# Layer 0's scans: from tiles of 2 states x 64 channels to tiles of 4 states x 32 channels, with steps and source rows through DRAM

## The chip, the core and the metric

The kernel is one launch on one core of a Trainium2 chip. TensorE (PE), VectorE (DVE), ScalarE (ACT) and GpSimd (POOL) compute; SyncE (SP) issues every DMA, in program order. The metric is the device time of the launch in microseconds.

## What is computed

A two-layer network in fp32 on `x` of 2 x 2048 x 256. Layer 0 adds to x a selective scan and a mixture of experts, both of the normalised x. Layer 1 adds two Mamba directions with a feed-forward part, and a butterfly network. The scan of layer 0, cut to what matters:

```python
z, params = x @ W_z.T, x @ W_params.T                # e = 256 channels, n = 16 states, r = 64
dt = softplus(params[..., :r] @ W_dt.T + b_dt)       # one step width per time and channel
u = silu(causal_conv(x))                             # per time and channel
A = -exp(A_log)                                      # channel x state
A_tilde = exp(dt[..., None] * A)
B_tilde = where(abs(A) < 1e-5, dt[..., None], (A_tilde - 1) / (A + 1e-10))
h[t+1] = A_tilde[t] * h[t] + B_tilde[t] * u[t]       # one scan per channel and state
y = einsum('bln,blen->ble', C, h)
out = ((y + u * D) * silu(z)) @ W_out.T
```

## The kernel before, in words

**Order.** All work is written as small operations `op(engine, us, f, deps, key, takes)`. A planner (`Plan.order`) sorts them once, at build time, into one order for each engine, from the keys, the costs written beside each operation, ring sizes (`rings`) and PSUM banks (`BANKS`). On the chip each engine then runs its list in order, and so does SyncE with its DMAs: a DMA that waits for a buffer or for a result holds all later ones. `key` counts scans; layer 0 has 32 keys to a chunk.

**Layer 0.** Time is cut into chunks of 512 steps (`T`), four for each of two batches, so eight chunks. Beside the scans of a chunk run the preparation of the next (`prepare`), the gates (`gates`), the output product (`finish`), and, spread over all chunks, the prologues, eight passes of experts (`experts`: gather at L773 and L782, first product L817, second L851, way back L898) and two chains of butterfly products on POOL and DVE.

A chunk's scans work on tiles of 128 partitions x 512 steps, 2 states x 64 channels each. An index `j` from 0 to 15 names a pair of such tiles (`h` = 0, 1), so a chunk has 32 scans. Each pair goes through these steps:

- two DMAs of 64 partitions bring C's rows of the two states (`cb`, L1235), and one brings source factors (`Gm` from the DRAM tile `Gd`, L1239);
- ACT makes the decay exp(dt * A) (L1224) from `dt`, which lies twice in SBUF, once for each state of a tile;
- the source: the recurrence is carried in a form in which the difference of u from step to step, times 1/A, enters (or dt * u, where A is tiny). For one half of the channels (`e` = 0) it is a product on PE with 128 rows (L1251: 64 rows of differences, 64 of shifted dt * u) out of `dw`; for the other half ACT scales `dw` (L1257) and DVE adds `dv` times a factor (L1262);
- DVE scans (L1271); POOL copies the last column (`hn`, L1291) for the next chunk and multiplies by `cb` (L1295);
- PE adds the two states into the sum `y` (L1299): two products, each of 64 columns of the matrix `fold`.

`prepare` makes `par` (L953), `dt` (four products L977, ACT L983, softplus L1051), u (ACT L1030), dt * u (POOL L1073), differences (POOL L1082 and once more L1100) and shifted copies (ACT L1085, L1107). What the changed variable lacks (`lack`, PE L1187, DVE L1190, PE L1194) and u * D (`skip`, ACT L1175) start the sum in PSUM; `gated` (DVE L1311) ends it.

**Layer 1** has sixteen chunks of 64 scans with the same decay, scan, `keep` (`hc`, L2044), product (L2050) and collect (L2062).

Of the kernel before, what the change touches and what calls it, by code (L numbers as in the profile page):

```python
# [99 lines left out]
RING0, CB0, STAGE0, RELAY0, XN0, DT0, DW0, GM0, LEAD0, LOAD0, SOURCE0, PROD0, COLLECT0, AHEAD0 = 5, 3, 4, 2, 3, 3, 4, 2, 4, 6, 2, 1, 3, 4  # L100
EARLY0, GATE0, PREP0, FIN0, PRO0, EXP0, EXP1, BFLY0 = -2, (10, 15), (4,30), (4, 12), ((-1, 8), (4, 14)), (10,27), (122,21), ((8, 110), (114, 200))
# [3 lines left out]
ON_POOL = "RRRRRR"  # L105
BANKS = {"pp0":((3,4,5,6,7),3),"yacc0":((0,1,2),3),"pp":((4,5,6,7),2),"ab":((4,5,6,7),2),"yacc":((0,1,2,3),4)}
# [316 lines left out]
def layer0(tc, c, a, pl, pools, x1d, wupd, wdnd, bupd):  # L423
# [23 lines left out]
    def weights():  # L447
        def first():
            W["cw"] = wp.tile([P, 2, 4], F32, name="cw")
            nc.sync.dma_start(W["cw"], a["conv0"].rearrange("(k p) c -> p k c", p=P))  # L450
            W["wpar"] = wp.tile([P, 2, 112], F32, name="wpar")
            nc.sync.dma_start(W["wpar"], a["wpT"].rearrange("(k p) e -> p k e", p=P))
            W["wdt"] = wp.tile([64, 512], F32, name="wdt")
            nc.sync.dma_start(W["wdt"], a["wdtT"])
            W["bdt"] = wp.tile([P, 4], F32, name="bdt")
            nc.sync.dma_start(W["bdt"], a["dt0"])

        def scans():
            W["A"] = wp.tile([P, 4, NS], F32, name="A")
            nc.sync.dma_start(W["A"], a["A0"])  # L460
            W["As"] = wp.tile([P, 4, 8], F32, name="As")
            nc.sync.dma_start(W["As"], a["A0s"])
            W["D0"] = wp.tile([64, 4], F32, name="D0")
            nc.sync.dma_start(W["D0"], a["D0"])
# [11 lines left out]
        def exps():  # L476
            nc.scalar.activation(W["As"], W["As"], AF.Exp)
            nc.scalar.activation(W["A"], W["A"], AF.Exp)

        def inverse(A, name):  # L480

            n = A.shape[2]
            small = wp.tile([P, 4, n], F32, name=name + "small")
            nc.vector.tensor_scalar(small, A, 1e-5, None, ALU.is_lt)
            large = wp.tile([P, 4, n], F32, name=name + "large")
            nc.vector.tensor_scalar(large, small, -1.0, 1.0, ALU.mult, ALU.add)
            c1 = wp.tile([P, 4, n], F32, name=name + "c1")
# [5 lines left out]
            return c1, small  # L493

        def factors():
            c1, small = inverse(W["A"], "c")

            cf = W["cf"] = wp.tile([P, 4, NS], F32, name="cf")
            nc.vector.tensor_copy(cf[0:64], c1[0:64])
            nc.vector.tensor_copy(cf[64:P], small[64:P])  # L500
            fold = W["fold"] = wp.tile([P, 64], F32, name="fold")
            nc.vector.tensor_add(fold, c.ident[:, 0:64], c.ident[:, 64:P])
            W["Gd"] = c.dram.tile([P, 2, 8, P], F32, name="Gd")

        def rows():
            W["c1s"], W["smalls"] = inverse(W["As"], "r")
            nc.vector.tensor_scalar(W["As"], W["As"], -1.0, None, ALU.mult)

        def sources(h):

            if h == 0:
                W["G"] = fp.tile([P, 4, NS, 64], F32, tag="selT", name="G")
            G = W["G"]
            nc.vector.tensor_mul(
                G[:, h],
                W["fold"].unsqueeze(1).broadcast_to([P, NS, 64]),
                W["cf"][:, h].unsqueeze(2).broadcast_to([P, NS, 64]),
            )

        def store(h):  # L520
            nc.sync.dma_start(
                W["Gd"][:, h].rearrange("p m e -> p (m e)"),
                W["G"][:, h].rearrange("p n e -> p (n e)"),
            )

        def lacks():

            nc.vector.tensor_scalar(W["cf"][0:64], W["cf"][0:64], -1.0, None, ALU.mult)

        def turn():  # L530
            W["ps"] = c.pp()
            for h in range(4):
                nc.tensor.transpose(
                    W["ps"][0:16, h * P : (h + 1) * P], W["cf"][:, h], c.ident
# [32 lines left out]
        f = op(DVE, 2.0, factors, e, key=-38)  # L567
        M["As"] = op(DVE, 1.2, rows, e, key=-30)
        M["G"] = []
        for h in range(2):  # L570
            g = op(DVE, 2.6, lambda h=h: sources(h), f, key=-20 + 6 * h,
                   takes="selT" if h == 0 else ())
            st = op(SP, 0.1, lambda h=h: store(h), g, key=-20 + 6 * h)
            if h == 0:
                g0 = g
            g0.users["selT"].append(st)
            M["G"].append(st)
        k = op(DVE, 0.5, lacks, *M["G"], g, key=-1.9)
        t = op(PE, 0.2, turn, k, key=-1.8, takes="pp0")
# [7 lines left out]
    def prologue(b, q, k0, k1, keep=None):  # L587
# [9 lines left out]
        for h in range(2):  # L597
# [6 lines left out]
            def norm(h=h):  # L604
                v = S["x"][:, 2 * h : 2 * h + 2]
                c.normalize(v, v, *S["m", h], 2, nc.gpsimd if ON_POOL[5] == "R" else None)
# [3 lines left out]
            ns.append(op(*((POOL, 1.5) if ON_POOL[5] == "R" else (DVE, 1.7)), norm, m))  # L610
# [111 lines left out]
    def experts(b, ec, k0, k1, k2):  # L722
# [3 lines left out]
        for q in range(4):  # L726
# [42 lines left out]
            for k in range(2):  # L769
                def gather(q=q, k=k):  # L770
                    S["g", q, k] = c.pp()
                    for i in range(4):
# [3 lines left out]
                            S["pb", q][:, i].rearrange("p g e -> p (g e)"),  # L776
# [4 lines left out]
                def gathered(q=q, k=k):  # L781
                    nc.scalar.copy(  # L782
                        S["selT"][:, k].rearrange("p e g -> p g e")[:, 32 * q : 32 * (q + 1), :],
                        S["g", q, k].rearrange("p (g e) -> p g e", e=16),
# [5 lines left out]
                o = op(ACT, 1.01, gathered, g, fs[0])  # L790
# [130 lines left out]
    class Chunk:  # L921
        def __init__(self, b, ch):
            self.b, self.ch, self.first = b, ch, ch == 0
            self.dt, self.dw, self.y = {}, {}, {}
# [4 lines left out]
    def prepare(i, k0, k1):  # L929
# [28 lines left out]
        def project():  # L958
            nc.scalar.copy(ck.par, S["p"][0:112, :])
            ck.cd = c.dram.tile([NS, T], F32, tag="cd0", name="cd0", bufs=3)  # L960

# [9 lines left out]
        ck.t_dt = {}  # L971
        for h in range(4):
            def delta_mm(h=h):
                if h % 2 == 0:
                    ck.dt[h // 2] = ap.tile([P, 2, T + 1], F32, tag="dt", name="dt", bufs=rings["dt0"])
                S["d", h] = c.pp()
                nc.tensor.matmul(  # L977
                    S["d", h], W["wdt"][:, h * P : (h + 1) * P], ck.par[0:64, :],
# [3 lines left out]
            def delta(h=h):  # L982
                nc.scalar.activation(  # L983
                    ck.dt[h // 2][:, h % 2, 1:], S["d", h], AF.Identity,
                    bias=W["bdt"][:, h : h + 1],
                )

            m = op(PE, 0.98, delta_mm, par, *outs[:h - h % 2], takes=("pp0", "dt0") if h % 2 == 0 else "pp0")
            if h % 2 == 0:
                ck.t_dt[h // 2] = m  # L990
                inline("dt0", m)
                m0 = m
            elif h % 2:
                m.deps.append(m0)
            p.users["par0"].append(m)
            outs.append(op(ACT, 0.63, delta, m))
            m.users["pp0"].append(outs[-1])

# [7 lines left out]
        for e in range(2):  # L1006
# [18 lines left out]
            def silu_u(e=e):  # L1025
                if e == 0:
                    ck.uw = ap.tile([P, 4, T + 2], F32, tag="uw", name="uw", bufs=rings["uw"])
                for h in (2 * e, 2 * e + 1):
                    r = slice(64 * (h % 2), 64 * (h % 2) + 64)
                    nc.scalar.activation(ck.uw[0:64, h, 2:], S["c", e][r], AF.Silu)  # L1030

            o = op(ACT, 1.25, silu_u, o, *us, takes="uw" if e == 0 else (), table="silu")
# [5 lines left out]
        def edge():  # L1038
            uw = ck.uw
            if ck.first:  # L1040
                nc.gpsimd.memset(uw[:, :, 0:1], 0.0)
                nc.gpsimd.tensor_copy(uw[0:64, :, 1:2], uw[0:64, :, 2:3])
# [5 lines left out]
        def softplus():  # L1048
            for e in range(2):
                d = ck.dt[e]  # L1050
                nc.scalar.activation(d[:, :, 1:], d[:, :, 1:], AF.Softplus)  # L1051

        so = op(ACT, 2.05, softplus, *outs, table="softplus")
        ck.o_sp = so
# [1522 lines left out]
```

## Time and profile before

| | |
|---|---|
| median of 3 runs | 2833.63 us (2831.72 to 2835.28) |
| profiled execution, first to last instruction | 2826.7 us |
| what lies around it, by the median | 6.9 us |
| scans of layer 0, first start to last start | 56.8 to 869.7 us |
| mean granted TensorE clock | 0.966 |
| busy over the span | PE 2535.5, DVE 2339.7, ACT 2261.0, POOL 2353.5 us |
| DMA | 282.62 MB, mean 100 GB/s |

A group of the profile reads: line, engine, operation, out<-in by the program's names, partitions x elements, count | busy us, mean ns of one | idle time of the engine just before them, and what ended it. A window gives the busy time of each engine in a stretch, then the granted clock, the mean share of the 16 DMA engines in use and the GB/s. A wait names who waited, for whom, the sum in us, how often, and the longest.

### The profile page before, as it was taken

To read this page: it belongs to the slowest core of one execution; us is meant where nothing else is said; L and a number is where in the kernel's file an instruction comes from. 1 tells how busy PE (TensorE), PEld (TensorE's weight loads), DVE (VectorE), ACT (ScalarE), POOL (GpSimd) and SP (SyncE) were. 2 spreads that over 40 slices of the span, in tenths; PEclk is the share of its full clock that TensorE was granted. 3 is DMA by queue.
4 is the path that set the end of the run, shared out by engine and by line. 5 is a ranking of instruction groups with operands and counts; after the bars stand their busy time and mean duration, and the time that the engine had idled before them with its cause. 6 is when DMAs were issued, how large, how long until landed. Compare 5 with 4: busy or idle time off the path is not lost.

```text
span 2826.7 us, 42579 instructions
## 1 busy us (share of the span) xinstructions
PE 2535.5 (90%) x15008; PEld 1851.1 (65%) x15008; DVE 2339.7 (83%) x2545; ACT 2261.0 (80%) x3460; POOL 2353.5 (83%) x2253
## 2 busy tenths in 40 slices
PE   6767988889986989999999999999999999999996
PEld 2333444444433768787787777878878788787875
DVE  5645886669795889998999999989898898989884
ACT  5747876778875989998898888879889889887871
POOL 6967667886565999998998989989898998988893
PEclk9979999999997999999999999999999999999998
DMA  6445347755433122212222232321212212212221
GB/s 212 135 144 180 119 126 247 258 173 160 139 106 127 50 79 77 90 50 65 68 83 65 75 91 79 96 81 49 73 56 73 79 46 83 60 64 64 62 63 50
DMA packets 228261, 282.62 MB, mean 100 GB/s; under 512 B 22160, under 2 KB 170768, under 8 KB 226128
## 3 DMA queue, kind: packets, MB, share of 16 engines
q1 hardware_dynamic: 228048, 279.91, 31.4%
q8 instruction: 118, 1.93, 0.3%
q14 instruction: 95, 0.78, 0.1%
HBM read 221.38 MB, written 58.46 MB: 99 GB/s over the span
## 4 chain that ended last, share of the span: by engine, by line
PE 51%; DVE 16%; POOL 14%; issue 7%; ACT 7%; DMA 4%; SPq 1%; POOLq 0%; DVEq 0%; ACTq 0%
PE bank L2018 10%; PE bank L2062 8%; POOL a L2050 7%; DVE a L2031 6%; PE bank L2246 3%; PE bank L2203 3%; PE bank L2132 3%; PE bank L1672 3%; POOL a L1295 3%; PE bank L1701 3%; DVE a L1271 2%; PE bank L2314 2%; PE bank L1795 2%; PE bank L1299 2%; POOL bT L1944 2%
## 5 line engine op out<-in xcount | busy, mean ns | idle before, releaser
L2050 POOL TENSOR_TENSOR a<-a,cb 128x1024 f32<-128x1024 f32 x512 | 1217.1, 2377 | 30.0 <-DMA cb<-bcd 0.5
L2031 DVE TENSOR_TENSOR_SCAN a<-a,hc,bank 128x512 f32<-128x512 f32 x768 | 930.7, 1261 | 73.3 <-PE bank L2018 65.6
L2000 ACT ACTIVATE a<-dt,A 128x512 f32<-128x512 f32 x1024 | 678.6, 717 | 53.4 <-PE bank L2062 35.7
L2018 PE MATMUL bank<-ident,bT 128*128 128x128 f32 x4096 | 616.5, 276 | 33.4 <-DVE a L2031 22.2
L2018 PEld LDWEIGHTS bank<-ident,bT 128*128 128x128 f32 x4096 | 486.1, 142 | 182.7 <-issue 68.3
L2062 PE MATMUL bank<-ident,a 128*128 128x128 f32 x4096 | 567.2, 274 | 37.9 <-POOL a L2050 37.5
L2062 PEld LDWEIGHTS bank<-ident,a 128*128 128x128 f32 x4096 | 470.6, 141 | 77.5 <-POOL a L2050 55.0
L1942 ACT ACTIVATE bT<-dtuT,BT 128x512 f32<-128x512 f32 x640 | 424.6, 714 | 13.8 <-PE bank L2018 8.2
L2031 DVE TENSOR_TENSOR_SCAN a<-a,bank 128x512 f32<-128x512 f32 x256 | 295.0, 1202 | 43.0 <-PE bank L2018 39.3
L1295 POOL TENSOR_TENSOR a<-a,cb 128x1024 f32<-128x1024 f32 x128 | 302.4, 2363 | 10.3
L1944 POOL TENSOR_SCALAR bT<-dtuT,BT 128x512 f32<-128x512 f32 x384 | 272.3, 713 | 9.0 <-PE bank L2018 1.8
L1271 DVE TENSOR_TENSOR_SCAN a<-bank,hn,a 128x512 f32<-128x512 f32 x192 | 241.6, 1275 | 35.0 <-PE bank L1251 29.6
L1224 ACT ACTIVATE a<-dt,As 128x512 f32<-128x512 f32 x256 | 173.5, 717 | 22.4 <-PE bank L1299 15.9
L1299 PE MATMUL bank<-a,fold 128*64 128x512 f32 x512 | 148.8, 654 | 22.7 <-POOL a L1295 22.0
L2044 POOL COPY hc<-a 128x2 f32<-128x2 f32 x512 | 107.8, 210 | 73.5 <-DVE a L2031 72.9
L1291 POOL COPY hn<-a 128x2 f32<-128x2 f32 x128 | 26.4, 206 | 168.8 <-DVE a L1271 165.0
L1251 PE MATMUL bank<-dw,Gm 128*128 128x512 f32 x256 | 140.9, 650 | 12.7 <-ACT dw L1085 3.2
L2203 PE MATMUL bank<-xnT,wup 128*128 128x256 f32 x512 | 125.5, 387 | 16.9 <-DMA wup<-wupd 13.9
L2132 PE MATMUL bank<-wout,ygT 128*128 128x256 f32 x512 | 126.7, 381 | 3.6 <-ACT h L2323 3.3
L2246 PE MATMUL bank<-wdn,gff 128*128 128x256 f32 x512 | 128.9, 386 | 0.7 <-ACT yT L2295 0.6
L1672 PE MATMUL bank<-winz,xnT 128*128 128x512 f32 x256 | 124.7, 597 | 4.7 <-DVE zu L1726 2.6
L1701 PE MATMUL bank<-xnT,winx 128*128 128x512 f32 x256 | 122.7, 595 | 1.6 <-DVE zu L1726 1.5
(211 smaller groups left out, 4339.2 us busy)
## 6 DMA issues: line engine op xcount, KB each, us to landing
cb<-bcd SPq DMA_DIRECT2D x256, 256.0 KB, 3.2
xnq<-xnd SPq DMA_DIRECT2D x32, 512.0 KB, 4.5
cb<-cd SPq DMA_DIRECT2D x128, 128.0 KB, 3.0
f<-in_f_dram SPq DMA_DIRECT2D x32, 512.0 KB, 4.8
interd<-stage SPq DMA_DIRECT2D x64, 256.0 KB, 4.8
relay<-interd SPq DMA_DIRECT2D x64, 256.0 KB, 3.3
xnTd<-xnT SPq DMA_DIRECT2D x16, 512.0 KB, 4.4
Gm<-Gd SPq DMA_DIRECT2D x64, 128.0 KB, 2.9
```

The source lines that it names most:

```text
L1271: nc.vector.tensor_tensor_scan(v, R["x", h], v, 0.0 if ck.first else pv.hn[:, k, h : h + 1], ALU.add, ALU.mult,)
L1295: nc.gpsimd.tensor_mul(v, v, C["cb"].unsqueeze(1).broadcast_to([P, 2, T]))
L1942: nc.scalar.activation(t, ck.dtuT[:, q, :], AF.Copy, scale=v)
L1944: nc.gpsimd.tensor_scalar(t, ck.dtuT[:, q, :], v, 1.0, ALU.mult, ALU.mult)
L2000: nc.scalar.activation(R["a"][:, h], ck.dt[:, e0 + h], AF.Exp, scale=w["A"][:, e0 + h, n : n + 1],)
L2018: nc.tensor.transpose(R["b", h][:, q * P : (q + 1) * P], ck.bT[n, q][:, e * P : (e + 1) * P], c.ident,)
L2031: nc.vector.tensor_tensor_scan(v[:, step], v[:, step], b[:, step], 0.0 if ck.first else pv.hn[:, e, n : n + 1], ALU.mult, ALU.add,)
L2050: nc.gpsimd.tensor_mul(v, v, ck.cb[n].unsqueeze(1).broadcast_to([P, 2, T]))
L2062: nc.tensor.matmul(ck.y[e][:, tb * P : (tb + 1) * P], v[:, tb * P : (tb + 1) * P], c.ident, start=False, stop=(n == NS - 1), is_transpose= ...
L2132: nc.tensor.matmul(S["ps"][:, n * D : (n + 1) * D], ck.ygT[:, e, q * P : (q + 1) * P], ck.w["wout"][:, e, :], start=(e == 0), stop=(e == 3),)
L2203: nc.tensor.matmul(S["up", hp][:, j * 256 : (j + 1) * 256], FW["wup"][:, kk, hd * P : (hd + 1) * P], ck.xnT[:, kk, t0 : t0 + 256], start=( ...
L2246: nc.tensor.matmul(S["ps"][:, j * D : (j + 1) * D], S["g"][:, hd, j * P : (j + 1) * P], FW["wdn"][:, hd, :], start=(hd == 0), stop=(hd == 7),)
```

## The change

Layer 0's tiles become 4 states x 32 channels; a chunk still has 32 scans in 16 pairs, now half of the channels after the other (`e` = j // 8).

- `dt`, softplus, u and dt * u are made once for 128 channels, without the doubled halves. The chunk's `dt` is stored to a DRAM tile `dd`, and for each 32 channels loaded back four times over (`dr`). Differences and dt * u are stored to a DRAM tile `wd` and loaded back as 64-row pairs (`w4`). The shifted copies, the second subtraction and the DRAM tile `Gd` go; the factors `G` stay in SBUF.
- Every source is a product with 64 rows, two side by side on the two row halves (`source`); `scaled` and `rest` go.
- C's rows come in one DMA for four states, and serve two pairs.
- The collect takes two pairs at once, four products of 32 columns each into four parts of the bank.
- `skip` and the adding of `lack` move from ACT and PE to DVE.
- `keep` is left out in the last chunk of each sequence, in layer 0 and in layer 1.
- In the experts, the gather product reads `pb` with the expert outermost, and ACT writes `selT` from it in runs of eight.
- Banks and rings: six banks for layer 0's products and sources (`pp0`, `ab0`, up to four for sources), two for sums; `dt` one buffer, `dr` five, `w4` three; the preparation lies on keys 1 to 24.

The core of the diff:

```diff
-RING0, CB0, STAGE0, RELAY0, XN0, DT0, DW0, GM0, LEAD0, LOAD0, SOURCE0, PROD0, COLLECT0, AHEAD0 = 5, 3, 4, 2, 3, 3, 4, 2, 4, 6, 2, 1, 3, 4
-EARLY0, GATE0, PREP0, FIN0, PRO0, EXP0, EXP1, BFLY0 = -2, (10, 15), (4,30), (4, 12), ((-1, 8), (4, 14)), (10,27), (122,21), ((8, 110), (114, 200))
+RING0, CB0, STAGE0, RELAY0, XN0, DR0, W40, LEAD0, LOAD0, SOURCE0, PROD0, COLLECT0, AHEAD0 = 5, 3, 4, 2, 3, 5, 3, 4, 6, 2, 1, 3, 4
+EARLY0, GATE0, PREP0, FIN0, PRO0, EXP0, EXP1, BFLY0 = -2, (10, 15), (1,24), (4, 12), ((-1, 8), (4, 14)), (10,27), (122,21), ((8, 110), (114, 200))
-ON_POOL = "RRRRRR"
-BANKS = {"pp0":((3,4,5,6,7),3),"yacc0":((0,1,2),3),"pp":((4,5,6,7),2),"ab":((4,5,6,7),2),"yacc":((0,1,2,3),4)}
+ON_POOL = "RR"
+BANKS = {"pp0":((2,3,4,5,6,7),3),"yacc0":((0,1),2),"pp":((4,5,6,7),2),"ab":((4,5,6,7),2),"ab0":((2,3,4,5,6,7),4),"yacc":((0,1,2,3),4)}
+            W["As"] = W["A"][:, 96:P].rearrange("p (g m) -> p g m", m=4)
+            W["D0"] = wp.tile([P, 2], F32, name="D0")
...
+            W["As"] = W["A"][:, 96:P].rearrange("p (g m) -> p g m", m=4)
+            fold = W["fold"] = wp.tile([P, 32], F32, name="fold")
+            W["G"] = wp.tile([P, 64, 32], F32, name="G")
...
-                            S["pb", q][:, i].rearrange("p g e -> p (g e)"),
+                            S["pb", q][:, i].rearrange("p g e -> p e g"),
...
-                        S["selT"][:, k].rearrange("p e g -> p g e")[:, 32 * q : 32 * (q + 1), :],
-                        S["g", q, k].rearrange("p (g e) -> p g e", e=16),
+                        S["selT"][:, k, :, 32 * q : 32 * (q + 1)].rearrange("p e (i g) -> p i e g", g=8),
+                        S["g", q, k].rearrange("p (i e g) -> p i e g", e=16, g=8),
-                o = op(ACT, 1.01, gathered, g, fs[0])
+                o = op(ACT, 0.6, gathered, g, fs[0])
...
+            ck.dd = c.dram.tile([D, T], F32, tag="dd0", name="dd0", bufs=3)
+            ck.wd = c.dram.tile([8, 2, 32, T], F32, tag="wd0", name="wd0", bufs=3)
...
+            nc.scalar.activation(ck.dt[:, :, 1:], ck.dt[:, :, 1:], AF.Softplus)
...
+        ck.o_dd = op(
+            lambda: nc.sync.dma_start(ck.dd.rearrange("(e p) t -> p e t", p=P), ck.dt[:, :, 0:T]),
+            ed,
+        )
...
+        def delta_u():
+            nc.gpsimd.tensor_mul(ck.uw[:, 2:4, 2:], ck.dt[:, :, 1:], ck.uw[:, 0:2, 2:])
...
-                (nc.gpsimd if ON_POOL[1 + e] == "R" else nc.vector).tensor_mul(
-                    ck.uw[64:P, s, 2:], ck.dt[e][0:64, :, 1:], ck.uw[0:64, s, 2:]
-                (nc.gpsimd if ON_POOL[3 + e] == "R" else nc.vector).tensor_sub(dw[0:64], ck.uw[0:64, s, 1 : T + 1], ck.uw[0:64, s, 0:T])
-                nc.scalar.copy(ck.dw[e][64:P], ck.uw[64:P, s, 0:T])
-                    nc.gpsimd.tensor_sub(
-                        ck.dw[1][64:P], ck.uw[0:64, s, 1 : T + 1], ck.uw[0:64, s, 0:T]
-                    nc.scalar.copy(ck.dv[64 * h : 64 * h + 64], ck.uw[64:P, s, 0:T])
+            def keep_v(e=e):
+                nc.sync.dma_start(ck.wd[4 * e : 4 * e + 4, 1], ck.uw[:, 2 + e, 0:T])
+
+            def step_u(e=e):
+                S["dd", e] = ap.tile([P, T], F32, tag="step", name="step", bufs=rings["step0"])
+                nc.gpsimd.tensor_sub(S["dd", e], ck.uw[:, e, 1 : T + 1], ck.uw[:, e, 0:T])
+
+            def keep_d(e=e):
+                nc.sync.dma_start(ck.wd[4 * e : 4 * e + 4, 0], S["dd", e])
...
+            def lack_mm(e=e, R=R):
+
+                for h in range(2):
+                    R[h] = c.pp()
+                for h in range(2):
+                    r = slice(64 + 32 * h, 80 + 32 * h)
+                    nc.tensor.matmul(R[h], W["cl"][r, e], ck.par[r, :], start=True, stop=True)
+
+            def lack_u(e=e, R=R):
                 ck.y[e] = c.yacc()
+                nc.vector.tensor_mul(ck.y[e], R[0], ck.uw[:, e, 1 : T + 1])
+
+            def skip(e=e):
+                nc.vector.scalar_tensor_tensor(
+                    ck.y[e], ck.uw[:, e, 2:], W["D0"][:, e : e + 1], ck.y[e], ALU.mult, ALU.add
+                )
+
+            def lack_v(e=e, R=R):
+                R["t"] = sp.tile([P, T], F32, tag="lk", name="lk", bufs=rings["lk"])
+                nc.vector.tensor_mul(R["t"], R[1], ck.uw[:, 2 + e, 1 : T + 1])
+
+            def lack_add(e=e, R=R):
+                nc.vector.tensor_add(ck.y[e], R["t"], ck.y[e])
...
-            m, e = divmod(j, 2)
-            k = 8 * e + m
+            e, g, jj = j // 8, j % 8 // 2, j % 2
+            jp = 2 * e + jj
...
+                def load_dt(h, jp=jp, Q=Q):
+                    Q["dt", h] = ap.tile([P, T], F32, tag="dr", name="dr", bufs=rings["dr0"])
+                    cg = 2 * jp + h
+                    nc.sync.dma_start(
+                        Q["dt", h],
+                        ck.dd[32 * cg : 32 * cg + 32].unsqueeze(0).broadcast_to([4, 32, T]),
+                    )
+
+                def load_w(jp=jp, Q=Q):
+                    Q["w"] = ap.tile([P, T], F32, tag="w4", name="w4", bufs=rings["w40"])
+                    nc.sync.dma_start(
+                        Q["w"], ck.wd[2 * jp : 2 * jp + 2].rearrange("g k p t -> (g k p) t")
+                    )
+
+                for h in range(2):
+                    Q["o_dt", h] = op(SP, 0.1, lambda load_dt=load_dt, h=h: load_dt(h), ck.o_dd,
+                                      takes="dr0", key=key - LOAD0 - 1 + h)
+                    inline("dr0", Q["o_dt", h])
+                Q["o_w"] = op(SP, 0.1, load_w, *ck.o_wd[e], takes="w40", key=key - LOAD0)
+                inline("w40", Q["o_w"])
...
+                def load(g=g, C=C):
+                    C["cb"] = sp.tile([P, T], F32, tag="cb", name="cb", bufs=rings["cb0"])
+                    nc.sync.dma_start(
+                        C["cb"],
+                        ck.cd[4 * g : 4 * g + 4].unsqueeze(1).broadcast_to([4, 32, T]),
+                    )
+
+                ld = op(SP, 0.1, load, ck.o_cd, takes="cb0", key=key - LOAD0)
+                inline("cb0", ld)
...
-            if e == 0:
-                C = {}
-
-                def load(m=m, C=C):
-                    C["cb"] = sp.tile([P, T], F32, tag="cb", name="cb", bufs=rings["cb0"])
-                    for j in range(2):
-                        nc.sync.dma_start(
-                            C["cb"][64 * j : 64 * j + 64], ck.cd[2 * m + j].partition_broadcast(64)
-                        )
-                    C["G"] = sp.tile([P, 2, P], F32, tag="G", name="Gm", bufs=rings["G"])
-                    nc.sync.dma_start(C["G"], W["Gd"][:, :, m, :])
-
-                ld = op(SP, 0.2, load, ck.o_cd, *M["G"], takes=("cb0", "G"), key=key - LOAD0)
-                inline("cb0", ld)
...
+            def source(g=g, jp=jp, R=R, Q=Q):
+                for h in range(2):
+                    R["x", h] = c.ab()
+                for h in range(2):
+                    r = slice(64 * h, 64 * h + 64)
+                    nc.tensor.matmul(
+                        R["x", h],
+                        W["G"][r, 16 * jp + 4 * g : 16 * jp + 4 * g + 4].rearrange("p n e -> p (n e)"),
+                        Q["w"][r], start=True, stop=True,
+                    )
+
+            s = op(PE, 1.0, source, Q["o_w"], M["G"], takes=("ab0", "ab0"), key=key - SOURCE0)
...
-                def source(h=h, R=R, C=C):
-                    R["x", h] = c.ab()
-                    nc.tensor.matmul(
-                        R["x", h], C["G"][:, h, :], ck.dw[0][:, h, :], start=True, stop=True
-                    )
-
-                def scaled(h=h, m=m, R=R):
-                    R["x", h] = c.ab()
-                    nc.scalar.activation(
-                        R["x", h], ck.dw[1][:, h, :], AF.Copy, scale=W["c1s"][:, 2 + h, m : m + 1]
-                    )
-
-                def rest(h=h, m=m, R=R):
-                    nc.vector.scalar_tensor_tensor(
-                        R["x", h], ck.dv[:, h, :], W["smalls"][:, 2 + h, m : m + 1], R["x", h],
-                        ALU.mult, ALU.add,
-                    )
-
...
+            if ck.ch < NT - 1:
+                kp = ck.o_keep[j] = op(POOL, 0.3, keep, before, key=key + 1 - PROD0)
...
-            def collect(e=e, m=m, R=R):
-                for h in range(2):
-                    nc.tensor.matmul(
-                        ck.y[e][64 * h : 64 * h + 64], W["fold"], R["a"][:, h], start=False,
-                        stop=(m == 7), skip_group_check=True,
-                    )
...
+                def collect(e=e, g=g, quad=quad):
+                    for q in range(4):
+                        nc.tensor.matmul(
+                            ck.y[e][32 * q : 32 * q + 32], W["fold"], quad[q // 2][0]["a"][:, q % 2],
+                            start=False, stop=(g == 3), skip_group_check=True,
+                        )
+
+                cl = op(PE, 1.05, collect, *prods, *ck.o_sum[e], key=key + 1 + COLLECT0)
...
+            self.last = k == (0 if self.bw else NT - 1)
+                if not ck.last:
+                    kp = op(POOL, 0.24, keep, sc[1], key=at + k + 1 - PROD)
```

## The prediction

> **What bounds the kernel now.** First the page's chain of work that ended last, then one window over the layer 0 stage (0 to 871 us; the last of its scans ends there) with two of its chunks.
>
> ```profile
> PE 51%; DVE 16%; POOL 14%; issue 7%; ACT 7%; DMA 4%; SPq 1%; POOLq 0%; DVEq 0%; ACTq 0%
> ```
> ```profile
> 0.00:871.00 871.00, 710.80 (x3088) 348.10 (x3088) 616.07 (x756) 640.04 (x976) 615.02 (x517) 0.93 0.52 165
> ```
> ```profile
> 500.00:603.00 103.00, 92.71 (x476) 49.63 (x476) 66.03 (x74) 84.03 (x124) 89.75 (x65) 1.00 0.70 227
> 603.00:709.00 106.00, 94.02 (x459) 50.81 (x460) 91.27 (x99) 89.58 (x148) 67.76 (x52) 0.95 0.54 171
> ```
>
> The columns are busy us of PE, PE weight loads, DVE, ACT and POOL, then the granted clock, the mean share of the 16 DMA engines and GB/s. The reader sees TensorE foremost (711 of 871) and on half of the chain, the other three near 620 to 640, and DMA at 0.52, at 0.70 in its fullest scan chunk: far from a limit while it is spread over 16 engines. Next the groups of 0 to 884 us, with the DMA totals of that window (packets, MB, share of 16 engines), the page's DMA sizes and SyncE's waits.
>
> ```profile
> L1299 PE MATMUL bank<-a,fold 128*64 128x512 f32 x512 | 148.8, 654 | 22.7 <-POOL a L1295 22.0 <-POOL xi L1713 0.5
> L1251 PE MATMUL bank<-dw,Gm 128*128 128x512 f32 x256 | 140.9, 650 | 12.7 <-ACT dw L1085 3.2 <-DVE a L1271 3.2 <-issue 2.4
> L1262 DVE SCALAR_TENSOR_TENSOR bank<-dv,rsmall,bank 128x512 f32<-128x512 f32 x128 | 94.5, 738 | 22.3 <-ACT bank L1257 22.1
> L1257 ACT ACTIVATE bank<-dw,rc 128x512 f32<-128x512 f32 x128 | 86.6, 686 | 29.0 <-DVE xacc L905 15.7 <-DVE a L1271 12.0 <-DVE lk L1190 0.7
> L898 PE MATMUL bank<-relay,PT 128*128 128x256 f32 x256 | 77.3, 433 | 40.0 <-DMA relay<-interd 30.4 <-DVE lt L658 4.6 <-DVE a L1271 2.4
> L773 PE MATMUL bank<-pb,xnq 128*128 128x128 f32 x512 | 69.6, 286 | 2.3 <-DVE a L1271 1.6 <-POOL pb L735 0.7
> L782 ACT COPY selT<-bank 128x512 f32<-128x512 f32 x64 | 65.8, 1055 | 16.4 <-PE bank L773 16.2
> L851 PE MATMUL bank<-f,inner 64*128 64x256 f32 x256 | 40.2, 420 | 2.2 <-DMA f<-in_f_dram 1.9 <-ACT stage L863 0.2
> ```
> ```profile
> q1 hardware_dynamic: 128784, 143.32, 51.1%
> ```
> ```profile
> cb<-bcd SPq DMA_DIRECT2D x256, 256.0 KB, 3.2
> ...
> cb<-cd SPq DMA_DIRECT2D x128, 128.0 KB, 3.0
> ```
> ```profile
> SPq L1235 <- POOL a L1295: 165.6, 40, 11.0
> ```
>
> Each fp32 product stands as two instructions. L851 (64 rows, issued in pairs) takes 40.2 us where L898, the same count and width, takes 77.3: two row halves run at once. L1299 (64 columns) has twice L1251's count in about its time: two column halves run at once. SyncE waits 165.6 us for buffers that POOL frees, and every later DMA queues behind such a wait.
>
> **The change, part by part.** Sums over layer 0 from these groups.
>
> PE: the collects are half as many groups of four 32-column products. Two at a time would save nothing of 148.8 us, four at a time half; I take 74, by L1299, where all column parts offered ran together. The lack sums (L1194, 22.8) go; the step products halve (L977, 35.7, so 18). Sources stay: 128 pairs with 64 rows for 128 full products. 74 + 23 + 18 = 115 us less: 596.
>
> ACT: L1257 (86.6), skip L1175 (22.0), the shifts L1107 and L1085 (25.0) go; L983, L1051, L1030 (56.4) halve; L782 writes runs of eight, 1.055 us becoming the 0.584 of L863 at best, so 0 to 30 less, taken 28. Sum 190: 450. DVE: L1262 (94.5) goes, 16 skips at the 0.747 of L1017 and 16 adds at the 0.678 of L905 come: 72 less, 544. POOL: three subtractions on 64 rows a chunk (45.5 in all) become 16 at L735's 1.292, two products (31.9) become 8 at L1295's 2.363, 32 copies of 0.206 go: 25 + 13 + 7 = 45 less, 570. If DMA stayed harmless every engine would gain.
>
> SyncE: per chunk 16 cb and 8 Gm issues go (24); 8 cb, 8 dt, 4 source-row loads and 5 stores come (25). Issue time cancels. But the dt loads wait for the decays to free five buffers, and the stores for POOL's steps; behind them queue relay, f and xnq loads, for which PE already stalls (30.4 us on the L898 row). At the start two landings (about 3.6 and 3.2 us, as of xnd and cb) enter the way to the first scan at 56.8; dt was ready at 44.2 and its first decay started at 53.1, so this is covered, and about 7 us if not.
>
> Layer 1: 128 copies `hc` of about 0.21 us leave POOL, 27 us in the last chunks. POOL is busy 1733 of 1943 us there, PE 1813, so most hides: between 0 and 27, I take 5.
>
> **DMA, the deciding term.** Bytes: the old cb, Gm and Gd (25 MiB) go; 8 dt stores of 512 KB and 32 source-row loads of 256 KB (12 MiB) come over all engines. The window moved 143.32 MB at 51.1% of 884 us, that is 452 us of each engine at 19.8 GB/s. At 317 GB/s of all sixteen that is 452 - 83 + 40 = 409 us of each. Then 64 dt loads, 64 cb loads and 32 stores of source rows, 160 in all, 256 KB each. Their patterns count 4 outermost (`broadcast_to([4, 32, T])`, and `wd[4 * e : 4 * e + 4, 1]`); the trace's big transfers count 64 or 128. No row shows how 4 is spread. One end: as cb<-bcd, over 16. Other end: over 4 engines, always the same ones. I take the second, because nothing in the pattern offers more than four equal parts, where 64 and 128 offer sixteen.
>
> Price on four engines (64 KB each). Low: from 128 KB (3.0 us) to 256 KB (3.2) is 0.2, so 0.4 for 256 KB on sixteen and 1.6 on four. By 19.8 GB/s: 3.3. High: 1024 KB bf loads land in 6.3 at best, (6.3 - 3.2) / 3 = 1.03 on sixteen, 4.1 on four. I take 2.7, below 3.3 because that mean has many packets under 512 B and these are 2 KB rows. 160 x 2.7 = 432. Those four then carry 409 + 432 = 841 us in a stage that lasts 871 today (665 to 1065 by the ends). They can't be full at every moment: at 0.74, the fullest window (0 to 57 us), 1136; at 1.0, 841. I take 0.91, an estimate for a limiting queue with many requests: 924, or 53 more than today. The gains above then don't show: PE, ACT and POOL idle on loads.
>
> The Trainium skill speaks against this change here: "DMA: Bandwidth & Descriptors", Rules for kernel authors, says that an outermost dimension below 16, a leading zero-stride broadcast above all, confines the whole DMA to at most that many engines, and another section (on why a DMA increments its semaphore by 16) that these are the lowest-numbered ones. No row here shows it or denies it. Its 27 GiB/s per engine would make 2.3 us of my 2.7, an estimate by that page: 409 + 362 = 771, at 0.91 847, 24 less than today.
>
> **Sum.** The profiled span is 2826.7, the median 2833.63; the 6.9 between is taken as what lies around the span, and stays. 2833.6 + 53 - 5 = 2882.
>
> **Rivals.**
> (A) Ends faster. The 160 transfers spread over sixteen engines: 160 x 256 KB at 317 GB/s is 132 us, 541 in all, share about 0.65, below the 0.70 that the 500 to 603 chunk bore without being longer. Then PE decides: 596 at today's 710.8 / 871 would be 730, a gain of 141. Half of it, 70, since stalls do not shrink with work: at 157.7 us PE ends an idle 23.4 us on an f load that SyncE issued only at 150.3, after a butterfly load that waited for POOL. 2833.6 - 70 - 5 = 2758, 2700 to 2810. It decides if the four-fold loads land in about 3.2 us.
> (B) A with a slower gather: the moving operand `pb` of L773 is now read 16 elements apart. No PE row reads with a gap. At full rate 0; at half rate 70 more (69.6 busy doubled), at a third 139. So 2828 to 2897, centre 2860, if DMA is harmless. For: eight columns of 64-byte gaps; against: nothing in the trace, which is why this end stays open.
> The Trainium skill, "SBUF — State Buffer", section on the DMA port swizzle, says that a step past a 16-byte line pays a penalty. No run here shows it; by that rule some of B's price falls due, by a full-rate read none.
>
> **How the numbers follow.** This kernel's measurement can tell about 0.2%, 5.7 us. Forecast 0.56 (its own range 2820 to 2960; 0.05 faster if packets run near the low price, 0.02 same, 0.49 slower). A 0.31 (0.29, 0.01, 0.01). B 0.13 (0.03, 0.01, 0.09). Faster 0.37, same 0.04, slower 0.59. Range 2750 to 2960: it leaves out the lower part of A (0.13) and the forecast's tail, prices near 3.3 (0.06).
>
> **What would show it.** Right: dr and cb loads of 256 KB landing in 6 us or more, other loads (relay, f, xnq) above their 3.3 to 4.8, PE idle on DMA before the back products (today L898) well over 30 us, layer 0's last scan near 925. Wrong: dr<-dd at 3.2 us with the last scan near 800 (A), or gather pairs at a longer pitch (B). The collects show four starts together, or the 74 us fails. The prediction fails too if SyncE's waits, not the engines behind it, hold the loads.

## The result and the profile after

The changed kernel takes 2944.86 us (median of 4 runs, 2941.79 to 2948.22) against 2832.68 (4 runs, 2829.71 to 2835.28): ratio 1.0405, 95% interval 1.0385 to 1.0425. That is 112 us slower, where 48 were forecast. The profiled span is 2946.5 us (before 2826.7).

Nearly all of it lies in layer 0. Its last scan ends at 988.0 us instead of 871.0, 117 us later; the scans of layer 1, first to last, take 1878.8 us instead of 1882.3. A further 8 us lie between the two: from layer 0's last scan to layer 1's first 20.9 us pass instead of 12.7. Layer 1's first chunk is now prepared too late: its softplus (L1828, before L1866) runs at 997.1 us, 9 us behind layer 0's last scan, where it ran at 849.8, 21 us ahead of its end. The wide kernels below have the same gap (20.6 and 20.7 us), the runs on the old tiles 12.2 to 12.4; the prediction has no term for it. The chain of work that ended last, from the page of the changed kernel:

```profile
PE 48%; POOL 13%; DVE 10%; DMA 7%; issue 5%; ACT 4%; SPq 0%; POOLq 0%; DVEq 0%; ACTq 0%
```

DMA has gone from 4% to 7% of it. The window over layer 0 (busy us of PE, weight loads, DVE, ACT, POOL, then granted clock, mean share of the 16 DMA engines, GB/s) and the DMA total of the same window (packets, MB, share):

```profile
0.00:988.00 988.00, 727.81 (x3200) 386.55 (x3201) 541.19 (x654) 442.53 (x726) 558.71 (x467) 0.83 0.57 174
```
```profile
q1 hardware_dynamic: 128320, 171.22, 56.3%
```

DVE, ACT and POOL fell as planned, but TensorE's busy time rose from 710.8 to 727.8 us, at a granted clock of 0.83 instead of 0.93. The DMA share, 0.57, looks harmless: it is a mean over sixteen engines, and hides what follows. The groups of 0 to 1020 us that answer to those of before:

```profile
L1223 PE MATMUL bank<-w,G 64*128 64x512 f32 x512 | 178.6, 716 | 31.5 <-DVE a L1237 17.7 <-DMA w<-wd 11.6 <-DVE zu L1688 1.0
...
L748 PE MATMUL bank<-pb,xnq 128*128 128x128 f32 x512 | 122.2, 399 | 4.9 <-ACT selT L757 3.8 <-ACT PT L729 0.7 <-issue 0.5
...
L873 PE MATMUL bank<-relay,PT 128*128 128x256 f32 x256 | 90.8, 497 | 96.9 <-DMA relay<-interd 90.1 <-DVE xacc L880 6.5 <-ACT a L1206 0.2
L1264 PE MATMUL bank<-a,fold 128*32 128x512 f32 x512 | 80.3, 680 | 0.8 <-POOL a L1252 0.8
...
L826 PE MATMUL bank<-f,inner 64*128 64x256 f32 x256 | 46.1, 457 | 24.6 <-DMA f<-in_f_dram 18.6 <-ACT stage L838 4.5 <-DVE bank L1130 1.6
...
L757 ACT COPY selT<-bank 128x512 f32<-128x512 f32 x64 | 37.4, 585 | 87.2 <-PE bank L748 87.2
```

The collects (L1264, before L1299) take 80.3 us instead of 148.8: four 32-column products start 6 or 7 ns apart and run together. The gather (L748, before L773) takes 122.2 instead of 69.6: its instructions follow each other at 0.218 us where they did at 0.111, so the moving operand is read at half rate. ScalarE's copy of it (L757) fell to 585 ns. And the back products (L873, before L898) now wait 90.1 us for their `relay` loads, before 30.4. Of the waits for DMA in the window of layer 0 (us in all, times, longest):

```profile
PE bank L873 <- DMA relay<-interd: 90.1, 18, 10.5
ACT a L1206 <- DMA dr<-dd: 64.0, 12, 14.1
...
POOL step L1053 <- DMA wd<-step: 31.4, 6, 7.1
```

The page shows no landing times for this kernel, but the trace has the completion records at the DMAs' semaphores. Each of the 1005 DMAs of the kernel before leaves 16 records at its semaphore. In the changed kernel the 160 four-fold transfers leave 5: one about 0.4 us after the end of the issue, four at the landing. Two transfers of the changed kernel, times in us:

```
cb load, four-fold, issue ends 31.27:   1 record at 31.7, 4 from 36.8 to 37.5
w load, 128 rows,   issue ends 60.60:  12 records from 62.5 to 62.9, 4 from 68.2 to 69.9
```

So a four-fold transfer is carried by four units, and of this wide one twelve parts land after 2 us while four land 5 to 7 us later. They are the same four units each time: where one narrow transfer was issued right behind another (58 such pairs in the changed kernel), the second landed 2.7 us after the first in the median, 2.9 in the mean, so they took turns. Landings from these records (issue to last record, median us):

| load or store | before | after | `e1_wide` |
|---|---|---|---|
| cb<-cd | 3.0 (128 KB) | 8.3 (256 KB) | 3.2 |
| dr<-dd | none | 10.9 | 4.9 |
| w<-wd (wide in both) | none | 10.4 | 4.9 |
| relay<-interd | 3.3 | 5.7 | 3.5 |
| interd<-stage | 4.8 | 7.6 | 5.7 |
| xnq<-xnd | 4.5 | 8.6 | 5.6 |

The shortest landing of a four-fold load is 4.7 us, that of the same loads made wide 2.6 and 2.7. The issuing engine shows it too. The instructions that issue the `dr` loads, in the view of their line (ns min/median/max), changed kernel and then `e1_wide`, where the loads are wide:

```profile
L1170 SPq DMA_DIRECT2D dr<-dd x64: 507/548/5067, 52.1 to 943.3; - x64
```
```profile
L1178 SPq DMA_DIRECT2D dr<-dd x64: 513/536/1424, 49.3 to 777.3; - x64
```

An issue normally takes about half a microsecond. In layer 0 of the changed kernel 115 of 500 DMA issues took over 1 us, the longest 9.1, and all issues together 435 us; before it was 9 of 496, 1.9 and 252 us. SyncE issues in order, so everything behind a held issue is late as well.

### The profile page after: what moved, and what is told of

Same layout as the page of the kernel before. It is cut to its first block, busy times and chain, and to the rows that moved or that the text cites. A ratio compares the mean times of both kernels' runs of the same rounds, so it can differ in the third digit from the quotient of the medians.

```text
span 2946.5 us, 42411 instructions
## 1 busy us (share of the span) xinstructions
PE 2564.1 (87%) x15164; PEld 1895.9 (64%) x15164; DVE 2265.7 (77%) x2445; ACT 2074.3 (70%) x3228; POOL 2273.9 (77%) x2075
## 4 chain that ended last, share of the span: by engine, by line
PE 48%; POOL 13%; DVE 10%; DMA 7%; issue 5%; ACT 4%; SPq 0%; POOLq 0%; DVEq 0%; ACTq 0%
PE bank L1980 9%; PE bank L2026 8%; POOL a L2012 8%; DVE a L1993 4%; PE bank L2210 4%; PE bank L2096 3%; DMA relay<-interd 3%; PE bank L2167 3%; PE bank L1634 3%; PE bank L1663 3%; POOL bT L1906 2%; PE bank L2278 2%; PE bank L1757 2%; PE bank L873 2%; DMA interd<-stage 1%
## 5 line engine op out<-in xcount | busy, mean ns | idle before, releaser
L2026 PEld LDWEIGHTS bank<-ident,a 128*128 128x128 f32 x4096 | 471.0, 142 | 75.5 <-POOL a L2012 52.6
L1206 ACT ACTIVATE a<-dr,A 128x512 f32<-128x512 f32 x256 | 171.5, 715 | 152.4 <-PE bank L1264 78.6
L1223 PE MATMUL bank<-w,G 64*128 64x512 f32 x512 | 178.6, 716 | 31.5 <-DVE a L1237 17.7
L873 PE MATMUL bank<-relay,PT 128*128 128x256 f32 x256 | 90.8, 497 | 96.9 <-DMA relay<-interd 90.1
L1248 POOL COPY hn<-a 128x2 f32<-128x2 f32 x96 | 19.5, 203 | 172.9 <-DVE a L1237 167.4
L873 PEld LDWEIGHTS bank<-relay,PT 128*128 128x128 f32 x256 | 58.2, 244 | 139.2 <-issue 65.5
L880 DVE TENSOR_TENSOR xacc<-xacc,bank 128x512 f32<-128x512 f32 x64 | 43.3, 680 | 122.7 <-PE bank L873 111.6
```

The lines of the kernel that those rows point to most:

```text
L2026: nc.tensor.matmul(ck.y[e][:, tb * P : (tb + 1) * P], v[:, tb * P : (tb + 1) * P], c.ident, start=False, stop=(n == NS - 1), is_transpose= ...
```

## Experiments

Three theories stood at first. N: the narrow transfers cost most. G: the gather's half rate costs most. S: SyncE's order and the new round trips through DRAM cost most, whatever the width. The first four runs are the two suspects crossed, and the gather alone on the old kernel.

**`e1_wide`: the transfers made wide.** Partition order (channel, state), so that 32 channels are outermost:

```diff
-ck.dd[32 * cg : 32 * cg + 32].unsqueeze(0).broadcast_to([4, 32, T]),
+ck.dd[32 * cg : 32 * cg + 32].unsqueeze(1).broadcast_to([32, 4, T]),
-ck.cd[4 * g : 4 * g + 4].unsqueeze(1).broadcast_to([4, 32, T]),
+ck.cd[4 * g : 4 * g + 4].unsqueeze(0).broadcast_to([32, 4, T]),
-ck.wd = c.dram.tile([8, 2, 32, T], ...)      # store ck.wd[4 * e : 4 * e + 4, 1]
+ck.wd = c.dram.tile([D, 2, T], ...)          # store ck.wd[P * e : P * e + P, 1]
 # G, fold and the columns of A0 reordered to match
```

> The changed kernel with the 160 four-fold transfers made wide and nothing else: same number, same bytes, same issue order. Partitions stand as (channel, state) instead of (state, channel), so the loads of steps and of the C row count 32 outermost and the source rows are stored and read in rows of 128. Theory N (four DMA engines are the bound): the four engines held 512 us of narrow and 428 us of other packets, 0.95 of 988 us; spread, every engine holds 556 us, no bound, and TensorE decides with its slow gather still in: 2820 to 2865 us, loads dr and cb landing in about 3.5 us. Theory G (the gather's half rate costs most, TensorE bound): wide loads give little, 2915 to 2945. Theory S (SyncE's order and the round trips through DRAM, whatever the width): 2910 to 2945, with landings shorter but the same waits.

Measured: 2781.56 us, ratio to before 0.9828 (0.9811 to 0.9845). The window to its last scan:

```profile
0.00:823.00 823.00, 694.83 (x3201) 371.82 (x3202) 535.84 (x655) 441.22 (x726) 558.70 (x467) 0.90 0.65 209
```

Same bytes, same 500 issues, 163 us less, and 38 us below the low end of N's range. All transfers now leave 16 records, the longest `dr` issue is 1.4 us, and the DMA share has risen to 0.65 without harm. TensorE's wait for `relay` is back at its size before, 30 us, and ScalarE's for `dr` falls from 64 to 17:

```profile
PE bank L881 <- DMA relay<-interd: 29.7, 13, 8.5
ACT a L1214 <- DMA dr<-dd: 16.8, 5, 4.7
```

S fails: order and round trips are all still there. G, which gave wide loads little, fails as the main cost.

**`e2_gather`: the gather of before in the changed kernel.**

```diff
-S["pb", q][:, i].rearrange("p g e -> p e g"),
+S["pb", q][:, i].rearrange("p g e -> p (g e)"),
 # and the copy to selT as before, in steps of 64 bytes
```

> The changed kernel with the gather of before (moving operand in a row, ScalarE's copy writing 64 bytes apart again); the 160 narrow transfers stay. Theory N: the four engines stay the bound; 0 to 20 us less, 2925 to 2945, although TensorE's busy time falls by 50. Theory G: most of 52.6 us comes back on TensorE's path, 2885 to 2900. Theory S: as N.

Measured: 2918.02 us, 26.8 less than the changed kernel (ratio to before 1.0309, 1.0293 to 1.0325). The gather's group is back near its old size, the back products still wait:

```profile
L873 PE MATMUL bank<-relay,PT 128*128 128x256 f32 x256 | 90.5, 496 | 108.3 <-DMA relay<-interd 88.6 <-ACT bft L1326 17.2 <-ACT a L1206 1.4
...
L748 PE MATMUL bank<-pb,xnq 128*128 128x128 f32 x512 | 78.1, 308 | 13.8 <-DMA xnq<-xnd 5.3 <-issue 5.3 <-DVE xacc L880 1.3
```

Between N (at most 20) and G (45 to 60). So the narrow transfers do not hide the gather's cost, as a full queue would: N's wording of a bound that covers everything else is wrong here.

**`e3_wide_gather`: both.**

> Both edits: wide transfers and the gather of before. Theory N, with the prediction's rival A: 2758, from 2740 to 2810, and the gather's half rate then shows its price as the difference to wide alone, 30 to 60 us. Theory G: 2850 to 2880. Theory S: 2890 or more.

Measured: 2751.78 us, ratio to before 0.9727 (0.9709 to 0.9745), the fastest kernel of this study and within N's range.

```profile
0.00:792.50 792.50, 644.15 (x3200) 332.05 (x3201) 529.09 (x655) 470.09 (x729) 559.35 (x467) 0.90 0.66 217
```

The four times make a square, and its sides agree:

| | gather in a row | gather 64 bytes apart | its price |
|---|---|---|---|
| wide | 2751.8 | 2781.6 | 29.8 |
| four-fold | 2918.0 | 2944.9 | 26.9 |
| price of four-fold | 166.2 | 163.3 | |

The two costs add. (The changed kernel was timed beside a kernel before of 2832.7 us, the other three beside one of 2829.4; taken by the ratios, its two differences are 27.2 and 163.3.) Without either, the rest of the change gains 2829.4 - 2751.8 = 78 us.

**`e4_before_gather`: the strided gather on the old kernel.** The edit of `e2_gather`, the other way round, in the kernel before.

> The kernel before with the changed gather alone (moving operand 16 elements apart, ScalarE's copy in runs of eight). TensorE's group goes from 69.6 to about 122 us, ScalarE's copy from 65.8 to about 37. If TensorE's busy time is the path in layer 0 (50% of the chain): 2870 to 2885. If its idle time takes the rest: 2845 to 2870. If both edits cancel: 2830 to 2840. No theory expects a gain.

Measured: 2838.09 us (10 runs, 2828.11 to 2846.17), ratio 1.0022 (1.0006 to 1.0039). The groups:

```profile
L773 PE MATMUL bank<-pb,xnq 128*128 128x128 f32 x512 | 120.3, 396 | 1.5 <-issue 1.2 <-ACT perm L684 0.2
...
L782 ACT COPY selT<-bank 128x512 f32<-128x512 f32 x64 | 37.2, 582 | 34.6 <-PE bank L773 34.3
```

TensorE pays 50.7 us, ScalarE gets 28.6 back, and the time moves by 6 us by the ratio (interval 2 to 11), 9 by the medians: the third expectation. The same edit costs 27 to 30 in the new schedule. The old one had ScalarE at 640 us of 871 and could use the relief; the new one has ScalarE at 441 and cannot. That this is the reason is argued, not shown.

**How the price depends on the number.** The next runs ask whether the four engines cost only when full (saturation), or each narrow transfer a little (theory L). Each run was timed beside its own runs of the kernel before; differences between runs of some 6 us lie within the intervals.

**`e5_cb_split`:** 64 of the 160 made wide by hand, in the changed kernel.

```diff
-nc.sync.dma_start(C["cb"], ck.cd[4 * g : 4 * g + 4].unsqueeze(1).broadcast_to([4, 32, T]))
+for n in range(4):
+    nc.sync.dma_start(C["cb"][32 * n : 32 * n + 32], ck.cd[4 * g + n].partition_broadcast(32))
```

> The changed kernel with each load of C rows issued as four loads of 32 partitions, one row each (64 issues become 256); the step loads and the stores of source rows, 96 transfers, stay narrow, the gather too. Theory N with saturation: the four engines then hold 307 us of narrow and 479 of other packets, 786 instead of 940; at the 0.95 of the changed kernel that ends layer 0 near 828, where the wide kernel ends (823), so most of the loss goes though 60% of the narrow transfers stay: 2785 to 2815. Theory L (each narrow transfer costs the same, 163.3 us over 160, wherever it stands): 64 of them make 65 us, 2880. If the 192 added issues hold SyncE's queue: above 2850.

Measured: 2874.02 us (ratio 1.0160, 1.0147 to 1.0173): 70.8 less, near L's 65, and 59 above saturation's range. By its number alone the third expectation, that the added issues hold SyncE's queue, would fit too; but SyncE's issues in layer 0 fell to 389 us in all, and `e10_all_split` below adds 480 issues for 25 us.

**`e6_wd_narrow` and `e12_wd_narrow_again`:** 32 narrow stores put into the fastest kernel.

```diff
-ck.wd = c.dram.tile([D, 2, T], ...)       # store ck.wd[P * e : P * e + P, k]
+ck.wd = c.dram.tile([8, 33, 2, T], ...)   # store ck.wd[4 * e : 4 * e + 4, 0:32, k]
 # the w load in two halves of 64 rows
```

> The fastest kernel so far (wide transfers, gather of before) with the 32 stores of source rows made four-fold again (and the loads of them in two halves, 32 more issues). Theory N with saturation: the four engines hold 102 us of narrow and 530 of other packets, 633 of the 793 us of layer 0, no bound: 2750 to 2765, against 2752. Theory L: 32 times 1.02 us, 2784.

The second run is the same kernel, made after the two of the next heading, whose prices its expectation cites:

> The kernel with the 32 narrow stores of source rows once more, for the size: the four earlier runs lay between 2773.2 and 2791.6, while 16 narrow stores of either kind cost 6.2 and 9.2 us against 2751.8. If the prices add up: 2767. If the four stores of a chunk queue on the same engines and so cost more together: 2780 to 2792.

Measured: 2788.43 us (ratio 0.9847, 0.9824 to 0.9869) and 2789.68 (0.9856, 0.9836 to 0.9876), 37 and 38 us over `e3_wide_gather`. The window of the first:

```profile
0.00:829.70 829.70, 654.74 (x3200) 338.45 (x3201) 531.92 (x655) 470.73 (x729) 559.32 (x467) 0.87 0.65 207
```

Its four engines carry (all packets less the narrow ones, over 16, plus the narrow ones over 4, at 100 ns a packet) 514 + 102 = 617 of 830 us. Far from full, and 1.1 to 1.2 us lost for each, as theory L has it. SyncE's issues are hardly held here (31 over 1 us, longest 2.6; `e3_wide_gather` 26 and 1.6): what remains is mainly the landing. The narrow stores land after 7.8 us (steps) and 8.4 (products) in the median, where the wide ones took 3.1 and 4.5.

**`e8_v_narrow` and `e9_step_narrow`:** half of these each; the other half stored in four parts.

```diff
-nc.sync.dma_start(ck.wd[4 * e : 4 * e + 4, 0:32, 0], S["dd", e])
+for n in range(4):
+    nc.sync.dma_start(ck.wd[4 * e + n, 0:32, 0], S["dd", e][32 * n : 32 * n + 32])
```

> As the kernel with 32 narrow stores (2788.4), but the 16 stores of steps are issued in four parts of 32 partitions, so only the 16 stores of products dt*u stay narrow. Two readings of the 36.7 us that 32 narrow stores cost against 2751.8. Theory C (chain): GpSimd's second step of a chunk waits for the store of the first to land, as they share one buffer, so the step stores alone cost: 2752 to 2764 here. Theory L (each narrow transfer delays whatever queues behind it, about 1.1 us): 2770.

> The converse: the 16 stores of steps narrow, the 16 of products in four parts. Theory C: 2780 to 2790. Theory L: 2770.

Measured: 2758.02 (ratio 0.9744, 0.9720 to 0.9768) and 2760.99 (0.9759, 0.9739 to 0.9778), so 6 and 9 us over `e3_wide_gather`, each hardly clear of the intervals. Theory C fits the first and fails at the second, the step stores alone do not carry it; L fails in its plain form, since 6 and 9 do not make 37. These two also have the padded DRAM tile and the split `w` loads of `e6_wd_narrow`, so those side edits do not carry its loss. Four narrow stores of a chunk together cost more than twice two. Where those further 22 us are lost is open; the traces point at the loads of `f`, for which the expert products on TensorE wait 7 us in `e3_wide_gather`, 19 and 6 in these two, but 37 and 30 in the two runs with all 32.

**`e10_all_split`:** all 160 issued in four parts of 32 partitions, 640 issues; the repair that needs no new layout.

> The changed kernel with each of its 160 four-fold transfers issued as four transfers of 32 partitions (640 issues), the gather still slow. If width alone counts: as the wide kernel, 2782 to 2800. If SyncE's 480 added issues (about 0.5 us each, 240 us of its queue in layer 0) count as well: above 2830.

Measured: 2806.26 us, ratio 0.9923 (0.9899 to 0.9947). Between the two expectations: 24.7 us above `e1_wide` for 480 more issues, 0.05 us each. SyncE's own time is cheap here; its 447 us of issues in layer 0 are as many as the changed kernel's 435, and that kernel is 139 us slower. So the time of SyncE's issues as such is not what costs. The DRAM layout is that of the changed kernel, so that is not it either.

**`e11_before_twofold`:** narrowness alone, on the kernel before.

```diff
-for j in range(2):
-    nc.sync.dma_start(C["cb"][64 * j : 64 * j + 64], ck.cd[2 * m + j].partition_broadcast(64))
+nc.sync.dma_start(C["cb"], ck.cd[2 * m : 2 * m + 2].unsqueeze(1).broadcast_to([2, 64, T]))
```

> The kernel before with one edit: the two loads of 64 partitions that fill a C tile become one load of both rows, two outermost (64 transfers of 256 KB instead of 128 of 128 KB, 64 issues fewer). If the outermost count sets the engines, each sits on two of them, 128 KB or 64 packets on each, 6.4 us at the 100 ns of a 2 KB packet, and lands in about 8 us or more; two engines then hold 410 us of it and 400 of other packets, of 871. By the price found on the changed kernel (1.02 us for each narrow transfer of 3.2 us, so about 2 for one of 6.4) 130 us more, 2960; by 1.0 each 2893. If narrowness cost only there, through the source rows' way over DRAM: no change or some us less for the issues saved, 2815 to 2830.

Measured: 2921.28 us, ratio 1.0326 (1.0301 to 1.0352), 91 us lost for 64 issues fewer, 1.4 us for each transfer, between the two prices expected (1.0 and 2). They leave 3 records each (one early, two at the landing), land after 8.3 us (median; shortest 7.0), and `relay` waits as in the changed kernel:

```profile
PE bank L898 <- DMA relay<-interd: 82.2, 15, 16.4
```

**`e7_keep`:** layer 1's edit alone, on the kernel before (`if not ck.last:` ahead of the copy `hc`).

> The kernel before with the one edit of layer 1: the last chunk of each direction and batch no longer copies its last column (128 copies, 27 us of GpSimd). The prediction took 5 us off, from 0 to 27. By the scans of layer 1 (1882.3 us from the first to the last before, 1878.8 after) it should be 2 to 6 us.

Measured: 2822.96 us (12 runs) against 2828.63, ratio 0.9981 (0.9972 to 0.9991): 5.7 us less.

## Why the prediction was right and wrong

**Right: the deciding term.** Four outermost means four engines; the 5 records against 16, the transfers that take turns and the square of four times show it. That the loads land in 6 us or more (8.3 and 10.9), that `relay`, `f` and `xnq` slow down and that the back products' wait goes well over 30 us (90.1) came as written. The Trainium skill's rule ("DMA: Bandwidth & Descriptors", Rules for kernel authors) agrees with the records on the count; which engines they are, no record here tells. By the landings an engine moved its 64 KB in 2.7 us, 24.5 GB/s; the mean over all 2 KB packets of layer 0, 100 ns, would be 20.5. Both are slower than the 27 GiB/s of that page from which I had 2.3 us a transfer.

**Wrong: the formula that priced that term.** The step that failed is the division of the four engines' load by a fill of 0.91. It makes the stage as long as a nearly full queue: below that, narrow transfers would cost nothing, and under it everything else would hide. The runs show neither. With the four engines 0.74 full (`e6_wd_narrow`) or, reckoned the same way, 0.88 full (`e5_cb_split`), each narrow transfer cost about 1.0 to 1.2 us, as much as in the changed kernel, and 16 narrow stores alone 6 to 9 us in all. Measured against rival A's kernel, this term was 163 to 166 us; I had 2882 - 2758 = 124. The inputs were closer. My 2.7 us for a transfer is the median between landings; by the mean packet it would be 3.2. The other traffic came to 431 us of each engine (with 3.2) or 451 (with 2.7), where I had 409. So the four engines carried 882 to 943 us instead of 841, 0.89 to 0.95 of the 988 that the stage took; as that share is taken from the measured end, it does not confirm the formula. What costs instead, as far as the landings and waits tell: a DMA is done only with its last part. The narrow transfers land 5 to 7 us later than wide ones, the wide ones beside them 2 to 6 us later, and the engines wait. In the changed kernel held issues come on top; no run separates the two there.

**Wrong: rival B was held to be an alternative.** I had its mechanism and its rate exactly (half: 0.218 us against 0.111), but gave it a price only "if DMA is harmless", as if a full queue would cover it. `e1_wide` to `e3_wide_gather` and the changed kernel to `e2_gather` make it 29.8 and 26.9 us: it adds with narrow transfers and without. Of the 64 us that the forecast lacks, this is 27. Its own price was too high, 70 for 27 to 30: the busy time grew by 44 to 53; that ScalarE's shorter copies and TensorE's idle time took the rest is argued, not shown. The Trainium skill's penalty for a step past a 16-byte line ("SBUF — State Buffer", the section on the DMA port swizzle) fits the half rate of TensorE's read here; the page gives no figure for it, and no run here tries another step.

**Rival A's number held.** 2758 was worked out for wide transfers and a harmless gather; that kernel, `e3_wide_gather`, takes 2751.8. That is in part luck. I took 115 us of TensorE's work away and let half of the gain through, 70 us of 141. In `e3_wide_gather` TensorE's work fell by 67 us only, from 711 to 644, and all of the gain came through: 644 at the share of before would end layer 0 at 789, and its last scan ended at 792.5. The gain of 78 less the 5.7 of layer 1 makes 72. The DMA share that I gave it, 0.65, is its 0.66.

**The smaller terms**, forecast and measured in the profiled run: DVE 544 and 541, ACT 450 and 443, POOL 570 and 559. On TensorE the collects fell to 80.3 (74 taken), the step products to 19.3 (18), the lack sums went. But the sources did not stay at 140.9: pairs of 64 rows took 178.6, and 165.5 in `e3_wide_gather`. With the gather (+52.6) and the lower clock (the back products 433 to 497 ns each) 596 became 728. Layer 1: 5 forecast, 5.7 measured (interval 3 to 8). The 8 us between the layers were not forecast. The start: I took two landings as covered, about 7 if not; the first scan moved from 56.8 to 63.5 in `e3_wide_gather`, the 7, and to 71.3 with narrow transfers.

**SyncE: "issue time cancels" failed.** 24 against 25 issues a chunk was right (496 and 500 in the stage), 252 against 435 us was not: issues were held. The wait that I expected SyncE to lose, for POOL's buffers, did shrink:

```profile
SPq L1193 <- POOL a L1252: 89.0, 26, 8.3
```

From 165.6 to 89.0 us, without any use.

## What to carry to other kernels

Read the outermost count of every DMA pattern: here a count of 4 put the whole transfer on four engines and a count of 2 on two, and the mean DMA share did not show it. Reorder the partitions so that the long axis is outermost, or split the DMA by hand; here that was worth 163 us of 2945 for no byte less, and 139 by hand. Do not assume that a bound covers a cost on another engine: "the bound covers it" was wrong on both sides of the square. The price of an edit depends on the schedule, though: the strided gather cost 27 to 30 us in the new kernel and 6 to 9 in the old.

## What was not expected of the hardware

SyncE's issues were held when narrow transfers were under way: up to 9.1 us for an issue of 0.4 to 0.6. In layer 0 of the changed kernel 11 of 152 issues took over 1 us with no narrow transfer under way, 58 of 105 with three or more. That full queues at the four engines hold the issue is inferred from this.

TensorE's granted clock in layer 0 was lowest where TensorE had the least to do. By busy share of the stage: 0.71 busy at 0.82 (`e2_gather`, to its last scan at 954.1 us), 0.74 at 0.83 (changed), 0.79 at 0.87 (`e6_wd_narrow`), 0.82 at 0.93 (before); the two wide kernels, 0.84 and 0.81 busy, had 0.90, so it is no strict order. If the idle time lowers the clock, a stall costs twice, once as idle time and once in slower products after it; no run here separates cause and effect.

Four products of 32 columns ran together at 680 ns, 646 in `e3_wide_gather`, as two of 64 did at 654.
